# A graph network layer on one core: silu and the exponentials made in another way, one tile in eight groups fetched row by row by SyncE

## The chip, the core and the metric

The kernel runs on one core of a Trainium2 chip, alone. The core has five engines that run side by side, each with its own queue of instructions in a fixed order: TensorE (PE, with PEld for its weight loads), VectorE (DVE), ScalarE (ACT), GpSimd (POOL) and SyncE (SP), which here only starts transfers. Semaphores make one engine wait for another. The metric is the time of one execution on the device in microseconds (us); smaller is better. The kernel before took 3901.85 us, the median of 3 runs (3901.23 to 3902.33).

## What is computed

A graph of 12,500 nodes with 64 features and 412,500 edges with 32 features, the edges sorted by receiver. The reference, cut to what matters:

```python
h = jnp.maximum(_layernorm(x, axis=-1), 0.0)
msg_in = concatenate([h[senders], h[receivers], edge_features], axis=-1)
messages = silu(msg_in @ W1 + b1) @ W2 + b2
att = softmax(silu(msg_in @ Wa1 + ba1) @ Wa2 + ba2, axis=0)     # over all edges
aggregated = segment_sum(messages * att, receivers, num_segments=12500)
return x + silu(concatenate([h, aggregated]) @ Wu1 + bu1) @ Wu2 + bu2
```

All is float32. The softmax runs over all edges at once, so the kernel keeps a running maximum and rescales what it has summed.

## The kernel before

**Nodes first.** The product of `[h[senders], h[receivers], edge] @ [Wa1 | W1]` is split. For each node the senders' part (128 numbers: 64 for attention, 64 for the message) is computed once and written to a table in DRAM, `ts_d`; the receivers' part with the bias goes to `tr_d`. These weights are halved beforehand (L248). The transposed features stay in SBUF as `hT`.

**Edges in groups.** An edge tile is 128 edges, a group is 8 tiles (`K`), and there are 403 groups (`NG`). For each edge, one row of `ts_d` has to be fetched by its sender. The loop over groups (L718 to L784) works on several groups at once; in iteration g:

- `load(g + 2)` (L504) prepares a later group. GpSimd fetches the senders' rows with one indirect transfer for each tile, 128 rows of 512 bytes, into the buffer `gs` (L513; seven such buffers). SyncE fetches every fourth group the edge features `eo` (L524) and receiver numbers `dbs` (L527, two transfers), and for every group a window of `tr_d` around the group's first receiver (`wins`, three buffers, L534, two transfers with an address from a register). VectorE compares the receivers with the rows of the window (L538), and TensorE makes receivers' part and edge part in PSUM, `pe` (L542, three buffers).
- In even groups from 8 to 390 the eighth tile isn't fetched by GpSimd. ScalarE collects it instead: 128 single columns of `hT`, each a copy of 4 bytes in 128 partitions whose address comes from a register (`columns`, L475 to L484), in bursts of 32 after one load of 32 numbers (L479). `burst(g, 0)` and `burst(g, 1)` (L486) give each iteration two bursts, 64 copies. SyncE fetches which half of the column counts (`half`, L472), VectorE masks (L547), and TensorE multiplies with the weights into `pe` (L548).
- `begin(g)` (L550): VectorE adds `pe` to `gs` (L553; in even groups the eighth tile is copied, L555), ScalarE takes the tanh of all 1024 columns (L556), written over `pe`.
- `end(g)` (L558): VectorE makes silu from it, (tanh + 1) times the sum, for the message half into `acts` (L566) and for the attention half (L572), multiplies the latter by `wa2` (L574) and sums to one logit for each edge (L577).
- Four groups make a batch. `top` (L585) finds the batch's maximum with a transpose on TensorE (L596), `weigh` (L599) updates the running maximum `nmax`, and ScalarE makes `scale`, the exponential of the change (L607), and `p`, the exponentials of the batch's logits with their sum (L610). `weigh` of a batch is called in the first iteration of the next one, after `burst(g, 1)` (L748).
- `sum_up` works on a group that lies at least five back: `by_node` (L614) builds for each tile a 128 x 40 matrix with `p` at each edge's receiver (L620, eight instructions) and TensorE sums the messages by receiver (L626); `out_of` (L632), `project` (L637) and `put` (L640 to L659) add the result to the sums of all nodes.

In the groups 16 to 119, beside this, thirteen tiles of nodes are prepared (`tile_bias`, `tile_bias_out`, `tile_rest`, L301 to L358). After the last group the sums become the output (L789 to L871).

**What sets the order.** Most instructions go through `pin`, which keeps an instruction behind the one written before it on the same engine. What isn't pinned (the loads of numbers into registers, most transfers on SyncE and the gathers) a scheduler places when the program is built, as early as it thinks that its inputs are there. What is pinned behind an unpinned load moves with it.

Of the kernel before, what the change touches and what calls it, by code (L numbers as in the profile page):

```python
# [9 lines left out]
I32 = mybir.dt.int32  # L10
# [34 lines left out]
WIDE = 128  # L45
EPS = 1e-5
# [313 lines left out]
def one_pass(tc, n_edges, v):  # L360
# [17 lines left out]
    with ExitStack() as ctx:  # L378
# [43 lines left out]
        with tc.tile_pool(name="work2", bufs=2) as work2, \  # L422
                tc.tile_pool(name="small", bufs=3) as small, \
                tc.tile_pool(name="pre_ps", bufs=AHEAD + 1, space=PSUM) as pre_ps, \
                tc.tile_pool(name="one_ps", bufs=1, space=PSUM) as one_ps:
            pes, gss, lgs, ps_, psums, sps, pps, ees, mts, nums, cols = ({} for _ in range(11))
# [12 lines left out]
            chosen = {g: i for i, g in enumerate(picks)}  # L439
            hT8 = v["hT"].rearrange("d b p -> d (b p)").bitcast(U8)  # L440
            sets = [(i, min(P, len(picks) - i)) for i in range(0, len(picks), P)]
# [3 lines left out]
            def places():  # L445
# [4 lines left out]
                for k, (i, n) in enumerate(sets):  # L450
                    e = (picks[i] * K + K - 1) * EP
                    nc.sync.dma_start(num[:n, k, :], bass.AP(
                        tensor=v["src_row"].tensor, offset=v["src_row"][:, e:].offset,
                        ap=[[EVERY * K * EP, n], [1, EP]]))
# [8 lines left out]
                for k, (i, n) in enumerate(sets):  # L463
                    nc.sync.dma_start(par_d[k * P:k * P + n, :], low[:n, k, :])
# [3 lines left out]
            def numbers(g):  # L468
                if g in chosen:
                    n = nums[g] = small.tile([P, EP], I32, name="half", bufs=3)  # L470
                    row = par_d[chosen[g]:chosen[g] + 1, :]
                    nc.sync.dma_start(n, bass.AP(tensor=row.tensor, offset=row.offset, ap=[[0, P], [1, EP]]))  # L472
                    cols[g] = small.tile([P, EP], F32, name="cols", bufs=3)

            def columns(g, first, n):  # L475
                if g not in chosen:
                    return
                to, i = cols[g].bitcast(U8), chosen[g]
                _, regs = nc.values_load_multi_w_load_instructions(  # L479
                    spots[i % P:i % P + 1, i // P, first:first + n], engines=[ENG.Activation],  # L480
                    min_val=HT_AT, max_val=HT_AT + 2 * NP - 4, skip_runtime_bounds_check_because=WHY)
                for i in range(n):
                    pin(nc.scalar.copy(to[:, 4 * (first + i):4 * (first + i) + 4],  # L483
                                       hT8[:, bass.ds(regs[i] - HT_AT, 4)]))  # L484

            def burst(g, k):  # L486
# [6 lines left out]
            tr_w = bass.AP(tensor=tr_d.tensor, offset=tr_d.offset,  # L493
                           ap=[[C, NP + WR - SHIFT], [SHIFT * C, 2], [1, C]])

            def registers(g, engine, at, base=base_sb, top=NP - 1):
                n = min(NQ, NG + (base is not base_sb) - g)
# [6 lines left out]
            def load(g):  # L504

                t = g * K
                if g % NQ == 0:
                    registers(g, ENG.SP, at_sp)
# [24 lines left out]
                for r in range(2):  # L533
                    nc.sync.dma_start(win[r * R:(r + 1) * R, :, r, :],  # L534
                                      tr_w[bass.ds(at_sp[g], R), :, :])
# [14 lines left out]
            def begin(g):  # L550

                n = K - (g in chosen)
                pin(nc.vector.tensor_tensor(gss[g][:, :n, :], pes[g][:, :n, :], gss[g][:, :n, :], ALU.add))  # L553
                if n < K:
                    pin(nc.vector.tensor_copy(gss[g][:, n, :], pes[g][:, n, :]))  # L555
                pin(nc.scalar.activation(pes[g], gss[g], AF.Tanh))  # L556

            def end(g, then=None):  # L558

                s = batch[g]  # L560
                if g == starts[s]:
                    lgs[s] = small.tile([EP, B * K], F32, name="lg")
                gs, th = gss.pop(g), pes.pop(g)

                def message():
                    pin(nc.vector.scalar_tensor_tensor(acts[g % ACTS][:, :, 0:U], th[:, :, U:C], 1.0,  # L566
                                                       gs[:, :, U:C], op0=ALU.add, op1=ALU.mult))

                if g < NG - 1:
                    message()  # L570
                att = th[:, :, 0:U]
                pin(nc.vector.scalar_tensor_tensor(att, th[:, :, 0:U], 1.0, gs[:, :, 0:U],  # L572
                                                   op0=ALU.add, op1=ALU.mult))
# [3 lines left out]
                pin(nc.vector.tensor_reduce(lgs[s][:, k:k + K], att, AX.X, ALU.add))  # L577
# [4 lines left out]
                if g == NG - 1:  # L582
                    message()

            def top(s):  # L585

                n = size[s] * K
                lg = lgs[s]
# [10 lines left out]
            def weigh(s):  # L599
# [5 lines left out]
                fall = small.tile([P, 1], F32, name="fall")  # L605
                pin(nc.vector.tensor_tensor(fall, nmax[:, s + 1:s + 2], nmax[:, s:s + 1], ALU.subtract))
                pin(nc.scalar.activation(scale[:, s:s + 1], fall, AF.Exp))  # L607
                p = ps_[s] = small.tile([EP, B * K], F32, name="p")
                psum = small.tile([EP, 1], F32, name="psum")
                pin(nc.scalar.activation(p[:, :n], lgs.pop(s)[:, :n], AF.Exp, bias=nmax[:EP, s + 1:s + 2],  # L610
                                         accum_out=psum))
                psums[s] = psum

            def by_node(g):  # L614
# [4 lines left out]
                for j in range(K):  # L619
                    pin(nc.vector.tensor_scalar(wt[:, j, :], iota_w[:EP, j // H, :],  # L620
# [503 lines left out]
```

## Time and profile before

| | |
|---|---|
| median of 3 runs | 3901.85 us |
| the profiled execution | 3904.89 us |
| its span, first to last instruction | 3903.1 us |
| mean granted TensorE clock | 0.642 of full speed |
| GpSimd: 3032 gathers (L513) | 2871.4 us busy |
| ScalarE: 24,576 column copies (L483) | 2415.5 us busy |
| VectorE: all | 3115.4 us busy |
| moved by the transfers | 391.30 MB, 100 GB/s |

Times in the profile are microseconds from the start of the span, or nanoseconds where a mean of one instruction is meant. A row of a group gives line, engine, operation, output and inputs with their shapes, how many; then busy time and mean time of one in ns; then how long the engine stood idle just ahead of them, and what ended that. "issue" means that nothing which the profile shows was waited for. Small instructions overlap, so busy time can be less than count times mean. A row of waits gives who waited for whom: total, times, longest. SPq and ACTq are the queues of SyncE and ScalarE: transfers being started, registers being loaded (TENSOR_LOAD) or computed (MOVE, FUSED_REGOPS).

### The profile page before, as it was taken

How to read it: one execution, taken by the hardware profiler on the slowest of the kernel's cores; microseconds unless marked ns; L12 is line 12 of the kernel's file. 1: busy time of each engine (PE TensorE's matmuls, PEld its weight loads, DVE VectorE, ACT ScalarE, POOL GpSimd, SP SyncE). 2: the span in 40 equal slices, each digit the busy share in tenths (PEclk: the TensorE clock that was granted, in tenths of full speed). 3: DMA queues.
4: the chain of work that ended last, by engine and by line, in shares of the span. 5: the costliest groups of instructions: out<-in, count | busy, mean ns of one | idle time of the engine just before them, and what ended most of it. 6: DMA issues, size and time to landing. Idle time of an engine off the chain costs nothing. (4 is left out here: it accounts for less than half of the span.)

```text
span 3903.1 us, 72226 instructions
## 1 busy us (share of the span) xinstructions
PE 2368.6 (61%) x11368; PEld 1927.2 (49%) x11368; DVE 3115.4 (80%) x8929; ACT 2954.1 (76%) x25797; POOL 2888.6 (74%) x3057
## 2 busy tenths in 40 slices
PE   6566656666666666665665656556565565555655
PEld 5454444454445554554444545445444454444545
DVE  6888787878788888887877877778777777877887
ACT  2887777777778888887877777878877878878712
POOL 3777777777777777777777777777777777777774
PEclk8766566666666657666666666666666666666666
DMA  7433334333433333333333333333333333333343
GB/s 280 114 104 94 102 100 106 94 104 99 107 93 97 97 97 91 94 97 94 87 97 85 97 93 89 97 86 97 93 88 97 86 96 91 90 97 86 95 116 86
DMA packets 228304, 391.30 MB, mean 100 GB/s; under 512 B 72369, under 2 KB 155762, under 8 KB 214770
## 3 DMA queue, kind: packets, MB, share of 16 engines
q0 software_dynamic: 97024, 198.90, 19.5%
q1 hardware_dynamic: 130802, 187.73, 17.9%
q14 instruction: 385, 3.15, 0.3%
q8 instruction: 93, 1.52, 0.2%
HBM read 360.52 MB, written 25.82 MB: 99 GB/s over the span
## 5 line engine op out<-in xcount | busy, mean ns | idle before, releaser
L513 POOL DMA_INDIRECT gs<-ts_d,src_sb x3032 | 2871.4, 947 | 973.1 <-issue 844.2
L483 ACT COPY cols<-hT 128x4 uint8 x24576 | 2415.5, 189 | 595.2 <-issue 594.2
L542 PE MATMUL pe<-wins,eo 128*128 128x256 f32 x3224 | 1470.7, 630 | 846.4 <-DVE eo L538 619.9
L542 PEld LDWEIGHTS pe<-wins,eo 128*128 128x128 f32 x3224 | 964.4, 316 | 1145.4 <-DVE eo L538 708.6
L620 DVE TENSOR_SCALAR wt<-iota_w,dloc,p 128x40 f32<-128x40 f32 x3224 | 726.9, 323 | 1.8
L553 DVE TENSOR_TENSOR gs<-pe,gs 128x1024 f32<-128x1024 f32 (+1 forms) x403 | 467.0, 1159 | 325.7 <-DMA gs<-ts_d,src_sb 303.3
L626 PE MATMUL sp<-wt,acts 128*65 128x40 f32 x6448 | 621.9, 268 | 4.6 <-DVE wt L620 3.5
L626 PEld LDWEIGHTS sp<-wt,acts 128*65 128x65 f32 x6448 | 586.0, 183 | 11.4 <-DVE wt L620 6.2
L556 ACT ACTIVATE pe<-gs 128x1024 f32<-128x1024 f32 x403 | 410.6, 1019 | 215.9 <-DVE gs L553 125.3
L637 PEld LDWEIGHTS mt<-ss,w2u 65*128 65x128 f32 x806 | 201.7, 281 | 330.4 <-issue 291.9
L637 PE MATMUL mt<-ss,w2u 65*128 65x40 f32 x806 | 183.7, 322 | 255.5 <-DVE gm L603 221.4
L566 DVE SCALAR_TENSOR_TENSOR acts<-pe,gs 128x512 f32<-128x512 f32 x403 | 277.6, 689 | 21.6 <-ACT pe L556 12.2
L574 DVE TENSOR_TENSOR pe<-pe,w_all 128x512 f32<-128x512 f32 x403 | 281.8, 699 | 13.5
L572 DVE SCALAR_TENSOR_TENSOR pe<-pe,gs 128x512 f32<-128x512 f32 x403 | 280.3, 696 | 10.5
L596 PE MATMUL mt<-ident,mx 128*128 128x128 f32 x107 | 46.7, 437 | 396.4 <-DVE sums L655 375.9
L577 DVE TENSOR_REDUCE lg<-pe 128x8 f32<-128x512 f32 x403 | 276.7, 687 | 10.5
L538 DVE TENSOR_SCALAR eo<-dbs,bj 64x256 f32<-64x256 int32 x806 | 275.5, 371 | 9.2
L596 PEld LDWEIGHTS mt<-ident,mx 128*128 128x128 f32 x107 | 19.2, 179 | 408.3 <-issue 404.5
L658 DVE COPY stand<-nmax 64x40 f32 x806 | 159.0, 197 | 3.4 <-issue 0.3
L547 DVE SCALAR_TENSOR_TENSOR cols<-half,cols 128x128 f32<-128x128 int32 x192 | 67.1, 349 | 100.6 <-ACT cols L483 98.5
L651 DVE SCALAR_TENSOR_TENSOR sums<-sums,scale,mt 64x40 f32 x214 | 54.4, 254 | 110.9 <-PE mt L637 107.4
L548 PEld LDWEIGHTS pe<-stack,cols 128*128 128x128 f32 x384 | 121.7, 317 | 32.5
(126 smaller groups left out, 957.6 us busy)
## 6 DMA issues: line engine op xcount, KB each, us to landing
eo<-in_edge_dram SPq DMA_DIRECT2D x100, 512.0 KB
dbs<-in_dst_row_dram SPq DMA_DIRECT2D x200, 256.0 KB
gs<-ts_d,src_sb POOLq DMA_INDIRECT x3032
wins<-tr_d SPq DMA_DIRECT2D x806, 32.0 KB
half<-par_d SPq DMA_DIRECT2D x192, 64.0 KB
ts_d<-ts SPq DMA_DIRECT2D x5, 896.0 KB
tr_d<-tr SPq DMA_DIRECT2D x5, 896.0 KB
hT_d<-hT SPq DMA_DIRECT2D x7, 448.0 KB
```

The costliest lines, as they stand in the source:

```text
L483: pin(nc.scalar.copy(to[:, 4 * (first + i):4 * (first + i) + 4], hT8[:, bass.ds(regs[i] - HT_AT, 4)]))
L513: nc.gpsimd.indirect_dma_start(out=full[:rows, j, :], out_offset=None, in_=ts_d[:, :], in_offset=bass.IndirectOffsetOnAxis(ap=src_full[:ro ...
L542: pin(nc.tensor.matmul(pe[:, 2 * q:2 * q + 2, :], eo[:, q * EP:(q + 1) * EP], win[:, q // 2, :, :], start=True, stop=q < H - 1 or g not in ...
L553: pin(nc.vector.tensor_tensor(gss[g][:, :n, :], pes[g][:, :n, :], gss[g][:, :n, :], ALU.add))
L556: pin(nc.scalar.activation(pes[g], gss[g], AF.Tanh))
L566: pin(nc.vector.scalar_tensor_tensor(acts[g % ACTS][:, :, 0:U], th[:, :, U:C], 1.0, gs[:, :, U:C], op0=ALU.add, op1=ALU.mult))
L572: pin(nc.vector.scalar_tensor_tensor(att, th[:, :, 0:U], 1.0, gs[:, :, 0:U], op0=ALU.add, op1=ALU.mult))
L574: pin(nc.vector.tensor_tensor(att, att, wa2[:EP, None, :].to_broadcast([EP, K, U]), ALU.mult))
L577: pin(nc.vector.tensor_reduce(lgs[s][:, k:k + K], att, AX.X, ALU.add))
L620: pin(nc.vector.tensor_scalar(wt[:, j, :], iota_w[:EP, j // H, :], dloc[:, g * K + j:g * K + j + 1], p[:, k + j:k + j + 1], op0=ALU.is_equ ...
L626: pin(nc.tensor.matmul(sp, acts[g % ACTS][:, j, :], wt[:, j, :], start=j == 0, stop=j == K - 1))
L637: pin(nc.tensor.matmul(pp, w2u.rearrange("s h u -> s (h u)"), sps.pop(g), start=True, stop=True))
```

## The change

- `begin` adds the gathered rows into `pe` in PSUM, so that the eighth tile needs no copy, and ScalarE makes silu itself with two instructions of 512 columns: attention into a new tile `att`, message into `acts`. The scale 2.0 undoes the halving. The two multiplications of `end` go.
- `weigh` gets the exponentials from tanh: with t = tanh(x / 32), exp(x / 16) = (1 + t) / (1 - t), and four squarings make exp(x), three on VectorE and the last on ScalarE, which also sums. The change of the maximum is one more column of the same instructions.
- `by_node` builds the matrix of all eight tiles in two instructions (compare, multiply).
- From group 15 on, in every eighth group up to 383 (47 groups, all odd), the last tile isn't gathered by GpSimd. SyncE fetches its 128 rows one by one into a tile `lone`, 16 rows in each iteration from 6 to 381, the last of them two iterations before the group begins. The numbers come into `ids` with a transfer, VectorE multiplies them by 512 (`scaled`), SyncE loads 16 of them into registers at once. All this is pinned. `begin` adds `lone` with an instruction of its own.
- The window's address is a byte offset too: `base_by` holds the first receivers times 512, and a row of the window's source is named by one register.
- A way to let VectorE collect columns as well (`vcolumns`, `spare_columns`, `vpicks`) is written but has nothing to do: `VRES` is empty, so its lists are. It is left out below.

```diff
+ROWS = 16
+ROW0 = 6
...
+            fetched = {}
+            for i in range(NG):
+                g = ROW0 + (EP * (i + 1) - 1) // ROWS + 2
+                if g < NG - 12:
+                    fetched[g] = i
+            order = list(fetched)
+            def ask(i):
+                if i < len(order):
+                    g = order[i]
+                    e = (g * K + K - 1 - (g in chosen)) * EP
+                    ids[i] = small.tile([1, EP], I32, name="ids", bufs=2)
+                    nc.sync.dma_start(ids[i], v["src_row"][:, e:e + EP])
+            def scaled(i):
+                if i < len(order):
+                    pin(nc.vector.tensor_scalar(ids[i], ids[i], 9, None, op0=ALU.logical_shift_left))
+            def fetch(g):
+                at = (g - ROW0) * ROWS
+                end = min(at + ROWS, len(order) * EP)
...
+                while 0 <= at < end:
+                    i, first = at // EP, at % EP
+                    n = min(end - at, EP - first)
+                    if first < ROWS:
+                        ask(i + 1)
+                    if EP // 2 <= first < EP // 2 + ROWS:
+                        scaled(i + 1)
+                    if first == 0:
+                        lone[order[i]] = small.tile([P, C], F32, name="lone", bufs=2)
+                    to = lone[order[i]]
+                    loads, regs = nc.values_load_multi_w_load_instructions(
+                        ids[i][0:1, first:first + n], engines=[ENG.SP], min_val=0, max_val=(NP - 1) * 4 * C,
+                        skip_runtime_bounds_check_because=WHY)
+                    for one in loads:
+                        pin(one)
+                    for k in range(n):
+                        pin(nc.sync.dma_start(to[first + k:first + k + 1, :].bitcast(U8),
+                                          ts8[bass.ds(regs[k], 4 * C)][None, :]))
+                    at += n
...
-                for j in range(K - (g in chosen)):
+                for j in range(K - (g in chosen) - (g in fetched)):
...
-                    nc.sync.dma_start(win[r * R:(r + 1) * R, :, r, :],
-                                      tr_w[bass.ds(at_sp[g], R), :, :])
+                    nc.sync.dma_start(win[r * R:(r + 1) * R, :, r, :].bitcast(U8),
+                                      tr_w[bass.ds(at_sp[g], 1)].rearrange("o r k f -> (o r) k f"))
...
             def begin(g):
-                n = K - (g in chosen)
-                pin(nc.vector.tensor_tensor(gss[g][:, :n, :], pes[g][:, :n, :], gss[g][:, :n, :], ALU.add))
-                if n < K:
-                    pin(nc.vector.tensor_copy(gss[g][:, n, :], pes[g][:, n, :]))
-                pin(nc.scalar.activation(pes[g], gss[g], AF.Tanh))
+                n = K - (g in chosen) - (g in fetched)
+                pe, gs = pes[g], gss.pop(g)
+                pin(nc.vector.tensor_tensor(pe[:, :n, :], pe[:, :n, :], gs[:, :n, :], ALU.add))
+                if g in fetched:
+                    pin(nc.vector.tensor_tensor(pe[:, n, :], pe[:, n, :], lone.pop(g)[:EP], ALU.add))
+                del pes[g]
+                att = atts[g] = silus.tile([P, K, U], F32, name="att")[:EP]
+                pin(nc.scalar.activation(att, pe[:, :, 0:U], AF.Silu, scale=2.0))
+                pin(nc.scalar.activation(acts[g % ACTS][:, :, 0:U], pe[:, :, U:C], AF.Silu, scale=2.0))
...
-                fall = small.tile([P, 1], F32, name="fall")
-                pin(nc.vector.tensor_tensor(fall, nmax[:, s + 1:s + 2], nmax[:, s:s + 1], ALU.subtract))
-                pin(nc.scalar.activation(scale[:, s:s + 1], fall, AF.Exp))
+                lg = lgs.pop(s)
+                pin(nc.vector.tensor_scalar(lg[:, n:n + 1], nmax[:, s:s + 1], -1.0, None, op0=ALU.mult))
+                part = small.tile([P, 1], F32, name="part")
+                pin(nc.vector.tensor_scalar(part, nmax[:, s + 1:s + 2], 1.0 / 32, None, op0=ALU.mult))
+                t, d = (small.tile([P, B * K + 1], F32, name=k)[:, :n + 1] for k in ("t", "d"))
+                pin(nc.scalar.activation(t, lg[:, :n + 1], AF.Tanh, bias=part, scale=1.0 / 32))
+                pin(nc.vector.tensor_scalar(d, t, -1.0, 1.0, op0=ALU.mult, op1=ALU.add))
+                pin(nc.vector.reciprocal(d, d))
+                pin(nc.vector.scalar_tensor_tensor(t, t, 1.0, d, op0=ALU.add, op1=ALU.mult))
+                for _ in range(3):
+                    pin(nc.vector.tensor_tensor(t, t, t, ALU.mult))
                 p = ps_[s] = small.tile([EP, B * K], F32, name="p")
-                pin(nc.scalar.activation(p[:, :n], lgs.pop(s)[:, :n], AF.Exp, bias=nmax[:EP, s + 1:s + 2],
-                                         accum_out=psum))
+                pin(nc.scalar.activation(p[:, :n], t[:EP, :n], AF.Square, accum_out=psum))
+                pin(nc.vector.tensor_tensor(scale[:, s:s + 1], t[:, n:n + 1], t[:, n:n + 1], ALU.mult))
...
-                for j in range(K):
-                    pin(nc.vector.tensor_scalar(wt[:, j, :], iota_w[:EP, j // H, :],
-                                                dloc[:, g * K + j:g * K + j + 1],
-                                                p[:, k + j:k + j + 1],
-                                                op0=ALU.is_equal, op1=ALU.mult))
+                at = dloc[:, g * K:(g + 1) * K].rearrange("p (r h) -> p r h", h=H)
+                pin(nc.vector.tensor_tensor(wt.rearrange("p (r h) w -> p r h w", h=H),
+                                            iota_w[:EP, :, None, :].to_broadcast([EP, 2, H, W]),
+                                            at[:, :, :, None].to_broadcast([EP, 2, H, W]), ALU.is_equal))
+                pin(nc.vector.tensor_tensor(wt, wt, p[:, k:k + K, None].to_broadcast([EP, K, W]), ALU.mult))
...
                 if g + AHEAD < NG:
                     load(g + AHEAD)
+                fetch(g)
                 numbers(g + 6)
```

More of the change, by code (lines that the diff above doesn't have):

```diff
@@ L45 @@
 WIDE = 128
+ROWS = 16
+ROW0 = 6
+VTURN = 4
+VRES = ()
+VSTART = 3
+VLATER = 6
+VBUFS = 2
 EPS = 1e-5
@@ new lines, in one_pass @@
+            order = list(fetched)
+            ids, lone = {}, {}
+            ts8 = ts_d.rearrange("n f -> (n f)").bitcast(U8)
+            def ask(i):
[7 more added lines that the diff above has]
+                    pin(nc.vector.tensor_scalar(ids[i], ids[i], 9, None, op0=ALU.logical_shift_left))
@@ new lines, in one_pass, with registers @@
+            at_sp, at_lo, at_hi, bus, rest = {}, {}, {}, {}, {}
+            row = 4 * C
+            tr8 = tr_d.bitcast(U8)
+            tr_w = bass.AP(tensor=tr8.tensor, offset=tr8.offset,
+                           ap=[[1, (NP - 1) * row + 1], [row, R], [SHIFT * row, 2], [1, row]])
+            base_by = keep.tile([1, NG + 1], I32, name="base_by")
+            nc.vector.tensor_scalar(base_by[:, :NG], base_sb[:, :NG], 9, None, op0=ALU.logical_shift_left)
+            def registers(g, engine, at, base, top):
+                n = min(NQ, NG + (base is not base_by) - g)
@@ L745, in one_pass @@
                     break
+                spare_columns()
+                vcolumns(g, 1)
                 end(g)
```

98 lines of the change are left out of this document (62 added, 36 removed).

## Prediction

> **What bounds the kernel now.** I read the page first, then the waits, then each engine's own rows. The first fence holds the page's span and busy shares, the gather line by itself (minimum, median and longest time, first and last start) and the waits of four engines (total, times, longest).
>
> ```profile
> span 3903.1 us, 72226 instructions
> PE 2368.6 (61%) x11368; PEld 1927.2 (49%) x11368; DVE 3115.4 (80%) x8929; ACT 2954.1 (76%) x25797; POOL 2888.6 (74%) x3057
> ...
> L513 POOL DMA_INDIRECT gs<-ts_d,src_sb x3032: 940/944/1352, 51.7 to 3846.0; - x190
> ...
> POOL gs L513 <- issue: 844.2, 2770, 0.3
> POOL gs L513 <- DMA gs<-ts_d,src_sb: 34.8, 114, 0.3
> ...
> ACT cols L483 <- issue: 594.2, 764, 1.3
> ACT pe L556 <- DVE gs L553: 125.3, 101, 9.6
> ...
> SPq L534 <- PE pe L542: 1251.2, 192, 10.7
> ```
>
> By busy share VectorE leads (80%), but it is GpSimd that never stops: no wait ahead of a gather is longer than 0.3, and "issue" means that nothing else held it. 3032 gathers start between 51.7 and 3846.0, (3846.0 - 51.7) / 3031 = **1.252 us each**. A usual pair of groups needs 15 of them, 9.39 a group. SyncE, in contrast, waits over 1251 for window buffers: it runs far ahead.
>
> The second limit is close. These rows are ScalarE's groups between 1250 and 1500, where it catches up with GpSimd:
>
> ```profile
> L483 ACT COPY cols<-hT 128x4 uint8 x1846 | 181.4, 189 | 35.3 <-issue 35.3
> L556 ACT ACTIVATE pe<-gs 128x1024 f32<-128x1024 f32 x29 | 29.4, 1014 | 0.0
> ```
>
> No wait for another engine is among them, so this is ScalarE at its own pace: 1846 copies are 28.8 groups of 64, and 250 / 28.8 = **8.67 a group**.
>
> **The change part by part.** *Gathers.* One tile leaves GpSimd in each group numbered 15, 23, ... 383, 47 in all. 47 x 1.252 = **58.8 us** less on the engine that sets the pace: 15 gathers a pair become 59 in eight groups, 9.23 a group.
>
> *Single rows.* The 47 x 128 rows go to SyncE, 16 in each of the groups 6 to 381, in its one queue with the windows, halves, edges and numbers. Its rows (minimum, median, longest; then timeline rows with start and time):
>
> ```profile
> L534 SPq FUSED_REGOPS  x806: 37/37/51, 88.1 to 3808.6; - x162
> L534 SPq MOVE wins<-tr_d x806: 29/29/38, 88.1 to 3808.6; - x162
> L534 SPq DMA_DIRECT2D wins<-tr_d x806: 316/317/1870, 88.2 to 3808.7; - x162
> ...
> L472 SPq DMA_DIRECT2D half<-par_d x192: 344/367/551, 94.8 to 3660.9; - x192
> ...
> L524 SPq DMA_DIRECT2D eo<-in_edge_dram x101: 471/481/1662, 79.2 to 3755.2; - x101
> ...
> L527 SPq DMA_DIRECT2D dbs<-in_dst_row_dram x202: 332/416/1281, 79.7 to 3755.8; - x101
> ...
> L498 SPq TENSOR_LOAD <-base_sb x101: 294/301/753, 87.2 to 3774.6; - x101
> ...
> L479 ACTq TENSOR_LOAD <-spots x768: 1942/2008/2800, 98.4 to 3706.6; - x192
> ...
> 7.80 0.31 SPq L148 DMA_DIRECT2D base_sb<-in_first_dram  x1
> ...
> 121.51 0.83 SPq L534 DMA_DIRECT2D wins<-tr_d  x2
> ...
> 3622.38 0.82 SPq L534 DMA_DIRECT2D wins<-tr_d  x2
> ...
> 500.97 1.30 SPq L349 DMA_DIRECT2D xt<-in_x_dram  x2
> ...
> 515.78 1.14 SPq L333 DMA_DIRECT2D bq_d<-bu  x2
> ```
>
> The one-row transfer of base_sb is the nearest to a single row: 0.31. The windows' pair (0.83 for two transfers, one FUSED_REGOPS and one MOVE) leaves about 0.04 between instructions. A single is then 0.31 + a MOVE 0.03 + two gaps: 0.41, as I take it; without the MOVE 0.35, with a FUSED_REGOPS 0.49. The offsets are now bytes, scaled beforehand, so that multiplication has nothing left to do, for the windows either. A group then costs SyncE 16 x 0.41 = 6.56; the load of 16 numbers, between 0.30 for 4 (L498) and 2.01 for 32 (L479), by a straight line 1.03, 1.07 with its gap; windows 0.89; half a half 0.23; a quarter of an edge load, two receiver loads and a number load, 0.49; an eighth of the ids 0.05. Sum **9.30** (8.3 and 10.6 at the two bounds), against 9.23 for GpSimd. SyncE's 1251 us of waiting are used up.
>
> What it is moved past: the windows of group g + 2 stand ahead of group g's rows, so they come late only by what SyncE is late in all. From its group 6 (121.51) to its group 381 (now at 3622.38, three groups ahead of use) it would need 375 x 9.30 = 3488, and some 45 more for the thirteen node tiles' transfers (a pair of xt 1.30, a pair of bq 1.14, one xb, each some 3.2): the windows of 383 go out at 3654, its last rows 9 later, and it can begin at 3665, as now (next fence, first row). GpSimd alone would let it begin at 3607.
>
> *The end.* The last 12 groups take 8 gathers each, 10.0 a group, while the others there are faster. First the tanh of group 383, then all engines from 3720 to 3870 (busy times of PE, PEld, DVE, ACT, POOL; the second last number is the busy share of the DMA queues):
>
> ```profile
> 3665.56 1.03 ACT L556 ACTIVATE pe<-gs 128x1024 f32<-128x1024 f32 x1 [0.37 <-DVE gs L553]
> ...
> 3720.00:3870.00 150.00, 81.06 (x448) 66.43 (x447) 122.15 (x393) 24.78 (x68) 98.60 (x104) 0.63 0.35 101
> ```
>
> VectorE is busy 122.15 for about 14 groups, 8.7 each, and loses some work below; I take 8. GpSimd is ahead by then, so from 383 on there are 7 groups at ScalarE's 8.8, 12 at 8 and 52 of ending (57 now from the last gather's start to the end, less 5 for its landing and addition), 210 instead of today's 238: 3665 + 210 = 3875.
>
> *Arithmetic.* The rows (times in ns of one, the second number behind the bar) that price the rest:
>
> ```profile
> L574 DVE TENSOR_TENSOR pe<-pe,w_all 128x512 f32<-128x512 f32 x403 | 281.8, 699 | 13.5
> L572 DVE SCALAR_TENSOR_TENSOR pe<-pe,gs 128x512 f32<-128x512 f32 x403 | 280.3, 696 | 10.5
> L566 DVE SCALAR_TENSOR_TENSOR acts<-pe,gs 128x512 f32<-128x512 f32 x403 | 277.6, 689 | 21.6 <-ACT pe L556 12.2
> L620 DVE TENSOR_SCALAR wt<-iota_w,dloc,p 128x40 f32<-128x40 f32 x3224 | 726.9, 323 | 1.8
> L555 DVE COPY gs<-pe 128x128 f32<-128x128 f32 x192 | 53.9, 281 | 0.0
> L831 ACT ACTIVATE mt<-hT 128x512 f32<-128x512 f32 x4 | 2.4, 597 | 1.8 <-POOL hT L826 1.6
> L556 ACT ACT_TABLE_LOAD x1 | 1.3, 1283 | 49.5 <-DVE gs L553 49.5
> L610 ACT ACTIVATE p<-lg,nmax 128x32 f32<-128x32 f32 x98 | 30.0, 306 | 0.0
> L607 ACT ACTIVATE scale<-fall 128x1 f32<-128x1 f32 x107 | 21.3, 199 | 33.7 <-DVE fall L606 33.7
> L589 DVE TENSOR_TENSOR lg<-lg,w_all 128x32 f32<-128x32 f32 x98 | 18.9, 193 | 3.3
> L208 DVE RECIPROCAL rstd<-rstd 128x14 f32<-128x14 f32 x5 | 1.2, 239 | 2.0 <-ACT rstd L203 1.9
> L208 DVE RECIPROCAL rstd<-rstd 128x8 f32<-128x8 f32 x2 | 0.4, 196 | 1.3 <-ACT rstd L203 1.3
> L691 DVE SCALAR_TENSOR_TENSOR total<-total,scale,psum 128x1 f32<-128x1 f32 x107 | 23.1, 216 | 15.4 <-ACT p L610 13.5
> ```
>
> VectorE loses the two multiplications of silu (0.69 + 0.70), half a copy (0.14) and eight small weights (726.9 / 403 = 1.80); it gains two of 320 elements (by L574's rate about 0.50 each), the lone tile and the scaling (0.28 each, an eighth). That is 2.3 less a group, before the weighing adds 0.4, and nothing on the path. ScalarE makes two silus of 512 (0.60 each, overlapping by 0.1) for one tanh of 1024 (1.01): 0.08 more a group, 8.75.
>
> *The weighing*, once in four groups, is where cover can go. Now two exponentials stand in a row on ScalarE and VectorE goes on. Afterwards tanh (behind a burst of 32 copies) is followed by seven VectorE operations and the Square waits for them: 0.19 + reciprocal of 33 (196 and 239 for 8 and 14 give 0.38) + 0.22 + 3 x 0.19, with 0.03 between, 1.55 us. Queued behind the waiting VectorE instruction is the next group's addition (1.2), for which the next silu waits: another 1.1 of ScalarE. Uncovered, 2.7 in four groups with the longer first activation, 0.7 a group: 8.75 + 0.7 = 9.45, over GpSimd's 9.23. What may cover it is the next burst of copies, which doesn't depend on any of this and isn't pinned behind it (each burst begins with a number load that is unpinned). That bursts do move ahead shows at the start:
>
> ```profile
> 98.98 1.03 ACT L556 ACTIVATE pe<-gs 128x1024 f32<-128x1024 f32 x1
> ...
> 102.78 3.13 ACT L483 COPY cols<-hT 128x4 uint8 x32
> ```
>
> That is a burst right behind the tanh of group 0, though the first that the program writes with anything to do belongs to group 4. I count the weighing at nothing, with 0.7 a group as its upper bound.
>
> *A rule weighed.* The row says 0.31 on SyncE for any transfer. The Trainium skill, "DMA: Bandwidth & Descriptors", section "Anatomy of one DMA", gives about 50 ns to a sequencer's dispatch (for GpSimd's path); by it, as an estimate, SyncE would need some 5 a group and the answer would be GpSimd's alone. No transfer of this trace was issued in that time, so I keep the row.
>
> **Forecast.** GpSimd alone ends at 3903.1 - 58.8 = 3844; SyncE's sum gives 3875. The profiled execution took 3904.89, 1.8 over its span and 3.0 over the median of 3901.85, so on the median these are 3843 and 3874. I forecast **3866**: faster by 0.9%, SyncE nearly the limit. Each 0.1 in SyncE's 9.30 is 37 us once it decides. Below 3843 only a quicker gather would help, for which nothing is changed; 944 ns is the median, 940 the least.
>
> **Rivals.**
> 1. *SyncE becomes the bound* and the kernel is slower. The price is its time per group, the place its queue, the point 9.38 a group, where 3875 becomes 3903. At 9.5, if it also waits 0.2 a group for its own earlier transfers (edge and receiver loads), 3949; with 0.49 a single 4350. For it: a sum with a margin of minus 0.07. Against: the unused 1251 us, and that it begins three groups ahead.
> 2. *ScalarE becomes the bound* through the uncovered weighing: 9.45 a group, 0.06 over today's 9.39, for 383 groups 23; 25 node tile steps, in which VectorE now has no lead left, about 1.5 each, 37; less 25 at the end: 3902 + 35 = 3937. It binds from 1.9 us of stall per weighing on, (9.23 - 8.75) x 4. A second form of it: if silu and tanh are not served by one table, two loads of 1283 (L556) per weighing, 2.6 more, give about 4000. The Trainium skill, "ScalarE: Activation LUTs", section "Table sets", lists tanh beside exp and sigmoid and says nothing of silu; this trace can't show it.
> 3. *The gain is lost in the queues*: the freed gathers come, but the others slow, since 6016 small rows share their 16 DMA queues. 2% on 1.252 is 75 us: 3918. Little speaks for it: queues 35% busy (the row from 3720), and 128 rows in eight groups replace as many.
>
> **How the numbers follow.** Forecast 0.48 (its own range 3840 to 3897), SyncE 0.26, ScalarE 0.17, lost gain 0.09. About 0.2%, 8 us, is what a measurement of this kernel can tell from no change. Of the forecast 0.44 is faster and 0.04 the same; of the rest 0.03 faster, 0.06 the same, 0.43 slower. So 0.47 faster, 0.10 same, 0.43 slower. The range reaches from 3838 to 3990, over the ScalarE case and SyncE up to 9.6; it leaves out SyncE well beyond, the table loads, and what is quicker than GpSimd.
>
> **What would show it.** 2985 gathers at 1.25, from about 52 to 3790; single rows at 0.41 and number loads near 1.0 on SyncE; ScalarE's copies between tanh and Square; VectorE near 2400 busy. I am wrong if GpSimd shows waits for buffers in the middle of the span, if the matrix products wait for windows, or if ScalarE stands idle ahead of each Square.

## The result, and the profile after

The changed kernel takes **4008.19 us** (median of 4 runs, 4006.39 to 4009.79), the kernel before 3902.09 beside it: a ratio of **1.027, 95% interval 1.026 to 1.028**. It is slower by 106 us; 3866 was forecast, in a range that ended at 3990. Two limits turned out to stand one behind the other: each weighing stops ScalarE, which sets the pace, and VectorE's new instructions hold up the gathers, which takes the gain away behind it. In some later sessions the kernel before itself took 5870 to 6020 us, and times measured there are not compared with the others.

First the page of the changed kernel, then from two more views its gather line (minimum, median and longest time, first and last start) and the waits of four engines (total, times, longest):

```profile
span 4004.7 us, 80328 instructions
...
PE 2294.9 (57%) x11368; PEld 1816.2 (45%) x11368; DVE 2368.1 (59%) x6464; ACT 2970.9 (74%) x26201; POOL 2914.7 (73%) x3010
```

```profile
L602 POOL DMA_INDIRECT gs<-ts_d,src_sb x2985: 938/944/1464, 52.0 to 3929.0; - x199
```

```profile
POOL gs L602 <- issue: 838.3, 2587, 49.6
POOL gs L602 <- DVE pe L643: 94.2, 83, 2.5
```

```profile
ACT cols L498 <- issue: 544.5, 763, 2.0
ACT att L648 <- DVE pe L643: 185.8, 125, 6.1
ACT p L705 <- DVE t L702: 175.6, 106, 3.2
```

```profile
DVE d L695 <- ACT t L693: 520.4, 104, 5.7
```

```profile
SPq L623 <- PE mt L733: 219.0, 89, 7.8
SPq L616 <- DVE eo L627: 197.0, 79, 13.0
```

VectorE lost a quarter of its work, and 47 gathers are gone, yet the last one starts 83 us later than before. GpSimd now waits 83 times for VectorE's addition, since that frees its buffers; before, once the gathers ran, no wait of it was longer than 0.3. Counted in the two traces at 2500, the gathers are six groups ahead of the additions now, with seven buffers, and were one group ahead before: GpSimd has stopped being the limit. New in ScalarE's list are 106 waits of the Square for the last squaring, 1.66 each, and 186 us ahead of the silu where 125 stood ahead of the tanh. SyncE still waits for others: it is not the limit.

One weighing, in the order of ScalarE's rows (start, time, what; idle time ahead and what ended it):

```profile
2411.56 0.59 ACT L648 ACTIVATE att<-pe 128x512 f32<-128x512 f32 x1
...
2420.09 0.59 ACT L648 ACTIVATE att<-pe 128x512 f32<-128x512 f32 x1
2420.58 0.58 ACT L649 ACTIVATE acts<-pe 128x512 f32<-128x512 f32 x1
2421.06 0.18 ACT L728 COPY ss<-sp 65x40 f32<-65x40 f32 x1
2421.45 3.14 ACT L498 COPY cols<-hT 128x4 uint8 x32 [0.21 <-issue]
2425.57 3.14 ACT L498 COPY cols<-hT 128x4 uint8 x32 [0.98 <-issue]
2428.62 0.32 ACT L693 ACTIVATE t<-lg,part 128x33 f32<-128x33 f32 x1
2430.64 0.23 ACT L705 ACTIVATE p<-t 128x32 f32<-128x32 f32 x1 [1.70 <-DVE t L702]
2430.78 0.19 ACT L705 ACTIVATION_READ_ACCUMULATOR p<-t 128x1 f32 x1
2432.28 0.60 ACT L648 ACTIVATE att<-pe 128x512 f32<-128x512 f32 x1 [1.32 <-DVE pe L643]
```

From silu to silu an ordinary group takes 8.5, this one 12.2. No copies stand between tanh and Square: both bursts are already through. VectorE's and GpSimd's rows of the same moment:

```profile
2428.97 0.32 DVE L695 TENSOR_SCALAR d<-t 128x33 f32<-128x33 f32 x1 [5.45 <-ACT t L693]
...
2431.02 1.23 DVE L643 TENSOR_TENSOR pe<-pe,gs 128x1024 f32<-128x1024 f32 x1 [0.21 <-DMA gs<-ts_d,src_sb]
```

```profile
2433.00 1.20 POOL L602 DMA_INDIRECT gs<-ts_d,src_sb  x1 [2.47 <-DVE pe L643]
```

VectorE stands idle for 5.45, because its first instruction of the second half waits for the tanh, which stands behind 32 copies; so the addition comes late, and GpSimd stands idle for 2.47 until it has its buffer. (The transfer named beside the addition can't be what it waited for: the gathers were six groups ahead.) Over the stretch from 1300 to 3500, behind the node tiles (means worked out from ScalarE's rows), ordinary groups take 8.49, groups with a weighing 12.12, and the one behind it 9.32, as its number load comes late: (2 x 8.49 + 12.12 + 9.32) / 4 = **9.60 a group**, for GpSimd's 9.39 before.

The second thing is in the gathers. By shape, with the mean time in ns behind the bar's comma, before and after:

```profile
L513 POOL DMA_INDIRECT gs<-ts_d,src_sb x3032 | 2871.4, 947 | 973.1 <-issue 844.2 <-DMA ts_d<-ts 49.3 <-DMA gs<-ts_d,src_sb 34.8
```

```profile
L602 POOL DMA_INDIRECT gs<-ts_d,src_sb x2985 | 2897.5, 971 | 1030.1 <-issue 838.3 <-DVE pe L643 94.2 <-DMA gs<-ts_d,src_sb 57.6
```

The median is 944 in both, but fewer gathers take more time in all. One of the long ones, and what VectorE does when it starts:

```profile
2613.76 0.94 POOL L602 DMA_INDIRECT gs<-ts_d,src_sb  x1 [0.30 <-issue]
2615.01 1.42 POOL L602 DMA_INDIRECT gs<-ts_d,src_sb  x1 [0.30 <-DVE wt L719]
2616.73 0.94 POOL L602 DMA_INDIRECT gs<-ts_d,src_sb  x1 [0.30 <-issue]
```

```profile
2614.52 0.49 DVE L719 TENSOR_TENSOR wt<-wt,p 128x320 f32<-128x320 f32 x1
2614.93 0.69 DVE L659 TENSOR_TENSOR att<-att,w_all 128x512 f32<-128x512 f32 x1
2615.65 0.69 DVE L662 TENSOR_REDUCE lg<-att 128x8 f32<-128x512 f32 x1
```

The multiplication of L659 still has 0.61 to run when the gather starts, and the gather takes 0.48 longer. The 390 gathers that start 0.05 or more after L659, L716 or L719 has begun, while it runs, follow one line: 0.944 plus what the instruction has left, less 0.1 (left 0.30 to 0.35: mean 1.147; 0.60 to 0.65: 1.430; less than 0.1: 0.944). They carry 53 of the 80 us that all gathers take over 0.944 each. Of the rest, 10 lie on 76 gathers that start within the first 0.05, of which most take their usual time, and 16 on the others, mostly those that start up to 0.5 ahead of L716. All three instructions read two operands from SBUF; before, the multiplication read silu from PSUM and each weight took one SBUF tensor and two scalars.

Which of the two sets the pace can be worked out: gathers of 0.971 with 0.305 between them need 7.375 x 1.276 = 9.41 a group, under ScalarE's 9.60. So the weighing is the limit here, and the slower gathers would be the next one.

### The profile page after: what moved, and what is told of

It reads as the page before. It is cut to its first block, busy times and chain, and to the rows that moved or that the text cites. A ratio compares the mean times of both kernels' runs of the same rounds, so it can differ in the third digit from the quotient of the medians.

```text
span 4004.7 us, 80328 instructions
## 1 busy us (share of the span) xinstructions
PE 2294.9 (57%) x11368; PEld 1816.2 (45%) x11368; DVE 2368.1 (59%) x6464; ACT 2970.9 (74%) x26201; POOL 2914.7 (73%) x3010
## 5 line engine op out<-in xcount | busy, mean ns | idle before, releaser
L631 PE MATMUL pe<-wins,eo 128*128 128x256 f32 x3224 | 1345.3, 590 | 1048.4 <-DVE eo L627 1010.4
L631 PEld LDWEIGHTS pe<-wins,eo 128*128 128x128 f32 x3224 | 917.2, 298 | 1291.7 <-DVE eo L627 1069.1
L643 DVE TENSOR_TENSOR pe<-pe,gs 128x896 f32<-128x896 f32 (+1 forms) x403 | 463.2, 1149 | 60.0 <-DMA gs<-ts_d,src_sb 39.6
L659 DVE TENSOR_TENSOR att<-att,w_all 128x512 f32<-128x512 f32 x403 | 277.5, 689 | 198.3 <-ACT att L648 197.9
L648 ACT ACTIVATE att<-pe 128x512 f32<-128x512 f32 x403 | 237.8, 590 | 192.7 <-DVE pe L643 185.8
L695 DVE TENSOR_SCALAR d<-t 128x33 f32<-128x33 f32 (+2 forms) x107 | 27.3, 255 | 520.4 <-ACT t L693 520.4
L662 DVE TENSOR_REDUCE lg<-att 128x8 f32<-128x512 f32 x403 | 275.0, 682 | 10.6
L649 ACT ACTIVATE acts<-pe 128x512 f32<-128x512 f32 x403 | 234.8, 583 | 0.0
L637 PE MATMUL pe<-stack,cols 128*128 128x128 f32 x384 | 106.0, 364 | 178.1 <-DVE cols L636 177.9
L719 DVE TENSOR_TENSOR wt<-wt,p 128x320 f32<-128x320 f32 x403 | 199.4, 495 | 13.9
L716 DVE TENSOR_TENSOR wt<-iota_w,dloc 128x320 f32<-128x320 f32 x403 | 195.1, 484 | 1.6
L705 ACT ACTIVATE p<-t 128x32 f32<-128x32 f32 (+2 forms) x107 | 24.3, 227 | 175.6 <-DVE t L702 175.6
```

Source lines behind the costliest of these rows:

```text
L631: pin(nc.tensor.matmul(pe[:, 2 * q:2 * q + 2, :], eo[:, q * EP:(q + 1) * EP], win[:, q // 2, :, :], start=True, stop=q < H - 1 or g not in ...
L643: pin(nc.vector.tensor_tensor(pe[:, :n, :], pe[:, :n, :], gs[:, :n, :], ALU.add))
L648: pin(nc.scalar.activation(att, pe[:, :, 0:U], AF.Silu, scale=2.0))
L649: pin(nc.scalar.activation(acts[g % ACTS][:, :, 0:U], pe[:, :, U:C], AF.Silu, scale=2.0))
L659: pin(nc.vector.tensor_tensor(att, att, wa2[:EP, None, :].to_broadcast([EP, K, U]), ALU.mult))
L662: pin(nc.vector.tensor_reduce(lgs[s][:EP, k:k + K], att, AX.X, ALU.add))
```

## The experiments

Theory **W**: ScalarE's stop at each weighing sets the pace. Theory **G**: the instructions with two SBUF operands slow the gathers. Rival **S**: the single rows, in SyncE's queue or beside the gathers, are the cause. Ratios are to the kernel before on the same chip, with 95% intervals.

**1. Tanh ahead of the second burst (early_tanh).**

```diff
                 end(g)
+                if batch[g] and g == starts[batch[g]] and weighed[0] <= batch[g] - 1:
+                    weigh_first(batch[g] - 1)
                 burst(g, 1)
                 if batch[g] and g == starts[batch[g]]:
                     weigh_upto(batch[g] - 1)
```

weigh_first holds the weighing up to the tanh, weigh_upto now the rest of it.

> The changed kernel with one thing moved: the tanh of a weighing goes out ahead of the second burst of copies, its Square stays behind it, so that VectorE's seven instructions between the two run beside 32 copies. Theory W (ScalarE waits at each weighing, 12.13 us for that group instead of 8.49, and the next number load comes late, 9.33): ScalarE falls to some 8.75 a group, and the time falls. How far tells W from W+G. Theory G (gathers of the changed kernel are slower, 971 ns in the mean for 947, because VectorE's new instructions with two SBUF inputs hold them up): GpSimd then needs 7.375 x 1.276 = 9.41 a group, as before, and the time is about 3910. W alone (gathers back at 1.252): 3845. Theory S (the single rows in SyncE's queue set the pace): unchanged, 4000 or more.

Measured: 3929.59, ratio 1.006 (1.005 to 1.008). ScalarE's waits ahead of the Square and VectorE's ahead of its first instruction fall from 175.6 and 520.4 to:

```profile
ACT p L715 <- DVE t L712: 18.9, 11, 3.0
```

```profile
DVE d L705 <- ACT t L695: 117.2, 98, 2.5
```

GpSimd hardly waits for buffers any more and sets the pace again, but its gathers still take 971 each:

```profile
L602 POOL DMA_INDIRECT gs<-ts_d,src_sb x2985 | 2899.5, 971 | 959.2 <-issue 899.1 <-DMA gs<-ts_d,src_sb 20.1 <-DVE mx L677 5.5
```

So W is worth 79 us here, and what is left, 3930 instead of 3845, is for G to explain. The groups now take 9.42 (1300 to 3500), as 7.375 gathers of 1.276 do.

**2. No large instruction with two SBUF operands (one_sbuf).**

```diff
-                att = atts[g] = silus.tile([P, K, U], F32, name="att")[:EP]
+                att = atts[g] = pe[:, :, 0:U]
...
-                pin(nc.vector.tensor_tensor(wt..., ALU.is_equal))
-                pin(nc.vector.tensor_tensor(wt, wt, p..., ALU.mult))
+                for j in range(K):
+                    pin(nc.vector.tensor_scalar(wt[:, j, :], iota_w..., dloc..., p...,
+                                                op0=ALU.is_equal, op1=ALU.mult))
```

> The changed kernel without large VectorE instructions that read two SBUF operands: the attention half of silu stays in PSUM, where it is multiplied, and the weights are made by eight instructions of one SBUF tensor and two scalars each, as before the change. The weighing stays as it is. Theory G: the gathers go back to 947 ns in the mean, and nearly none is over 1.05 us. The time: W says ScalarE still sets 9.6 a group, so 3990 to 4020 in spite of quick gathers. If G were the cause by itself, 3845 to 3870. Theory S: gathers stay slow, 4000.

Measured: 4433.59, 1.135 (1.133 to 1.137). The gathers are as G says, the time is a miss:

```profile
L602 POOL DMA_INDIRECT gs<-ts_d,src_sb x2985 | 2824.3, 946 | 1511.9 <-issue 905.1 <-DVE pe L643 532.5 <-DVE sums L751 49.7
```

```profile
2405.29 0.57 ACT L648 ACTIVATE pe<-pe 128x512 f32<-128x512 f32 x1
2405.90 0.60 ACT L649 ACTIVATE acts<-pe 128x512 f32<-128x512 f32 x1
2406.39 0.18 ACT L728 COPY ss<-sp 65x40 f32<-65x40 f32 x1
2407.95 3.14 ACT L498 COPY cols<-hT 128x4 uint8 x32 [1.38 <-issue]
2412.01 3.14 ACT L498 COPY cols<-hT 128x4 uint8 x32 [0.92 <-issue]
2415.06 0.57 ACT L648 ACTIVATE pe<-pe 128x512 f32<-128x512 f32 x1
```

The edit had a side effect. As both silus now work in one PSUM tile, the second waits for the first; the number load behind it starts only with the second silu (at 2405.91 in the trace) and, hidden but for 0.21 in the changed kernel, costs 1.38: an ordinary group is 9.8 instead of 8.5, before any weighing.

**3. Both edits (early_one_sbuf), and then the number loads pinned 20 copies early (best_p20).**

```diff
-                _, regs = spots_of(g, first, n, ENG.Activation)
+                regs = ahead.pop((g, first), None) or numbered(g, first, n)
+                at = calls.index((g, first, n))
                 for i in range(n):
+                    if i == n - 20 and at + 1 < len(calls):
+                        ahead[calls[at + 1][:2]] = numbered(*calls[at + 1])
```

numbered is the load with its instructions kept in program order, calls the list of bursts.

> Both edits together. W+G: GpSimd is the limit again with 7.375 gathers of 1.252, 9.23 a group: 3840 to 3860, faster than both kernels. If SyncE is the limit at the 9.3 of the prediction, 3875 or more. Theory S: 4000.

> The changed kernel with the early tanh and without the large instructions of two SBUF operands, and with ScalarE's number loads pinned 20 copies ahead of the burst that uses them. In the run with the first two edits alone the number loads had moved, so that ScalarE stood 1.38 and 0.92 us before the bursts of each group (9.87 a group for 8.5). If that is the only reason it was slow: ScalarE falls below 8.5 a group, GpSimd is the limit with 7.375 x 1.252 = 9.23, and the time is 3840 to 3860. If VectorE's longer chain (eight weights again, 2.6 us for 1.0) is the reason: 4000 or more.

Measured: 4114.88, 1.053 (1.051 to 1.055), and 3966.93, 1.015 (1.013 to 1.017). Both miss. The gathers take 945 and 946, but ScalarE sets the pace: the median group takes 9.87 and 9.43 (1300 to 3500). In best_p20 each of the two loads of a group costs 1.0, since only copies of 0.1 stand ahead of it:

```profile
2411.76 1.24 ACT L511 COPY cols<-hT 128x4 uint8 x12
2413.99 3.14 ACT L511 COPY cols<-hT 128x4 uint8 x32 [1.00 <-issue]
2418.11 2.00 ACT L511 COPY cols<-hT 128x4 uint8 x20 [0.98 <-issue]
```

These runs show G in the gathers, not yet in the time.

**4. The rows by themselves: the changed kernel without them (no_rows), the kernel before with nothing but them (rows_only).**

```diff
-                if g < NG - 12:
+                if g < 0:
                     fetched[g] = i
```

is no_rows; rows_only is the kernel before with the change's fetch(g), its byte addresses of the windows, and in begin(g)

```diff
+                if g in fetched:
+                    pin(nc.vector.tensor_tensor(gss[g][:, n, :], pes[g][:, n, :], lone.pop(g)[:EP], ALU.add))
+                    n += 1
```

> The changed kernel without the single rows: all 3032 gathers on GpSimd again, everything else as changed. W: ScalarE's 9.61 is above GpSimd's 7.5 x 1.276 = 9.57, so about the same, 4000 to 4015. Theory S: the rows were the cause, and without them the time falls to about 3910.

> The kernel before with one part of the change: the single rows on SyncE (47 tiles leave GpSimd) with the windows' addresses in bytes; tanh, exponentials, weights and their operands stay as before. Theory G+W: the gain of the rows is real, and what lost it came from the other parts. Gathers stay at 947 ns in the mean, 1.252 apart; GpSimd needs 9.23 a group, and the time is 3845 to 3875. If the rows themselves slow the gathers or SyncE is the limit: 3900 or more.

Measured: no_rows 4011.26, 1.027 (1.025 to 1.028), as the changed kernel; **rows_only 3859.81, 0.988 (0.986 to 0.990)**, faster than both kernels. S falls. (In no_rows GpSimd needs 7.5 x 1.280 = 9.60 a group, no more than ScalarE, so the 47 gathers that it has again don't show in the time.) The gathers of rows_only, by shape and between 2500 and 3000 (busy time and count):

```profile
L566 POOL DMA_INDIRECT gs<-ts_d,src_sb x2985 | 2824.2, 946 | 973.1 <-issue 896.5 <-DMA gs<-ts_d,src_sb 17.4 <-DVE wt L676 12.5
```

```profile
2500.00:3000.00 500.00, 377.99 (x401) 0.62 0.40 95
```

401 in 500 us, 1.25 each: in this stretch the rows beside them slow nothing.

**5. One instruction more with two SBUF operands (extra_two), and one with a single one (extra_one).** In the kernel with the early tanh, in a tile `idle` whose result nobody reads:

```diff
                 end(g)
+                pin(nc.vector.tensor_tensor(idle, dloc[:, :K * C], dloc[:, K * C:2 * K * C], ALU.add))
```

for extra_two, and for extra_one

```diff
+                pin(nc.vector.tensor_reduce(idle[:, :K], dloc[:, :K * C].rearrange("p (k c) -> p k c", k=K), AX.X, ALU.add))
```

> The kernel with the early tanh, and one more VectorE instruction a group whose result nobody reads: an addition of two parts of an SBUF tile, 128 x 1024, some 1.2 us. VectorE has 40% to spare. Theory G (a gather that is to start while such an instruction runs waits for its end, less 0.1): some 0.5 us a group more on GpSimd, gathers of 1.04 us in the mean, time some 4120. Without G: as the next kernel, 3920 to 3950.

> The control to the kernel with an additional addition: in the same place a sum over 128 x 1024 elements, with a single SBUF operand and about the same 1.2 us. Theory G: gathers as without it, 971 ns in the mean, and the time 3920 to 3950. If any longer VectorE work slows the gathers: as the addition, some 4120.

Measured: 4182.05, 1.071 (1.069 to 1.073), and 3924.83, 1.004 (1.003 to 1.006). VectorE's additional instruction and the gathers, of the first and then of the second:

```profile
L858 DVE TENSOR_TENSOR idle<-dloc 128x1024 f32<-128x1024 f32 x402 | 487.8, 1214 | 0.0
```

```profile
L603 POOL DMA_INDIRECT gs<-ts_d,src_sb x2985 | 3159.6, 1058 | 958.9 <-issue 916.4 <-DMA gs<-ts_d,src_sb 20.4 <-DVE t L713 14.0
```

```profile
L858 DVE TENSOR_REDUCE idle<-dloc 128x8 f32<-128x1024 f32 x402 | 485.1, 1207 | 0.0
```

```profile
L603 POOL DMA_INDIRECT gs<-ts_d,src_sb x2985 | 2908.9, 975 | 958.7 <-issue 890.4 <-DMA gs<-ts_d,src_sb 23.5 <-DVE att L660 8.0
```

The same 1.21 us on an engine with 40% to spare: 257 us dearer with two SBUF operands, and GpSimd's busy time shows 3159.6 - 2908.9 = 251 of them. It is also dearer than the 4120 expected. The two differ in one more thing: the addition writes 1024 numbers in each partition to SBUF, the sum 8. That the writing isn't the cause can be seen in rows_only, whose addition reads one operand from SBUF and one from PSUM, writes as much to SBUF and takes as long:

```profile
L606 DVE TENSOR_TENSOR gs<-pe,gs 128x1024 f32<-128x1024 f32 x164 | 200.8, 1224 | 80.1 <-DMA gs<-ts_d,src_sb 54.3 <-issue 21.1 <-PE pe L595 3.9
```

The 354 gathers that start while L606 runs, in either of its two sizes, take 0.944 in the mean, 0.961 at most. So extra_two and extra_one show G by itself, in the time.

**6. The weights in two steps by themselves (rows_wt2_c): rows_only, with the two tensor_tensor of the change for wt.**

> The kernel before with the single rows and the weights in two steps, once more, since in both runs so far the kernel before took some 6000 us. Theory G: gathers near 957 ns instead of 946, 0.08 to 0.12 a group, so 3890 to 3910 instead of the 3860 without the two steps, in spite of less work on VectorE; without G 3860 or less.

Measured: 3880.41, 0.995 (0.993 to 0.996): 21 us slower than rows_only, 27 by the two ratios, and less than the 30 to 50 that were expected. VectorE has 0.8 a group less to do (busy rows of 1.80 and 0.98). The gathers are as expected:

```profile
L566 POOL DMA_INDIRECT gs<-ts_d,src_sb x2985 | 2859.8, 958 | 960.3 <-issue 899.8 <-DMA gs<-ts_d,src_sb 20.8 <-DVE gs L611 8.6
```

**7. What stays open.** Three more edits were made: the early tanh with eight weights (early_wt8), and rows_only with 18 or 20 rows a group.

> The kernel with the early tanh, and the weights again in eight instructions with one SBUF tensor each; the attention half of silu stays in SBUF, where it is multiplied with two SBUF operands (0.69 us). Theory G: by the rule that a gather waits for the rest of the instruction, less 0.1, the two steps of the weights cost 2 x 0.39 x 0.39 / 2.5 = 0.12 of the 0.26 a group that the three cost together; so gathers near 957 ns in the mean instead of 971, GpSimd about 9.32 a group, and the time 3885 to 3900 instead of 3930. If the weights had no part in it: 3930 or more, since VectorE's chain is 1.6 us longer.

> The kernel before with 20 single rows a group instead of 16: 59 tiles leave GpSimd, 12 more. If SyncE still had room, 12 x 1.25 = 15 us are gained, 3845. By the rows of the run with 16, SyncE needs 8.35 a group (a single takes 0.32 with its MOVE, 16 numbers 1.15), and four more make 9.64, over GpSimd's 9.2: then SyncE is the limit and the time is 3950 to 4020, with matrix products that wait for windows.

> The kernel before with 18 single rows a group: 53 tiles leave GpSimd, 6 more than with 16. SyncE at 8.35 + 2 x 0.32 = 9.0 a group stays under GpSimd's 9.21: 6 x 1.25 = 7.5 us less than with 16 rows, about 3852. If SyncE needs 0.2 a group more than its own rows say, it is the limit by now: 3860 to 3900.

All their runs (three of early_wt8, three with 20 rows, one with 18), and two more of rows_wt2, fell into the sessions named with the result, so their times (6033 to 6051; 6519 to 6632; 6711; 5858 and 5869) say nothing of the usual kernel. What can be read there is the gather: 955 to 957 ns in three runs of early_wt8, as G expected, 949 and 951 in rows_wt2, less than the 957 expected, and 945 to 948 with 18 and 20 rows. With 20 rows the matrix products waited for windows there,

```profile
PE pe L595 <- DMA wins<-tr_d: 2633.5, 250, 18.6
```

so SyncE's transfers came late there. From how many rows on SyncE sets the pace in usual times isn't settled. How much of G belongs to the attention product and how much to the weights is shown in the time for the weights alone, by experiment 6. And no run shows in the time what the changed kernel would gain from quick gathers alone, since one_sbuf slowed ScalarE as well.

## Why the prediction was wrong

*What bounds the kernel, and the gathers.* Right. With the rows alone the kernel takes 3860. That this is 6 under the forecast of 3866 is in part luck: 3866 was taken between 3843 (GpSimd alone) and 3874, and the second came from a sum for SyncE that was too large. Of the 58.8 us, 48 arrive in the span (3903.1 to 3855.2). The rest goes at 13 gathers between 947 and 1180, while node tiles are prepared; GpSimd stands idle up to 3.0 ahead of them, 12.6 us in all beyond the usual 0.3. One of them in rows_only:

```profile
1102.36 0.94 POOL L566 DMA_INDIRECT gs<-ts_d,src_sb  x1 [3.00 <-ACT cols L485]
```

No such wait stands in the trace of the kernel before. What makes them late isn't shown.

*SyncE's sum.* The size was off: 9.30 a group was forecast, the rows add up to some 8.3 with the gaps between them (1300 to 3500).

```profile
L571 SPq MOVE lone<-ts_d x6016: 29/29/38, 117.0 to 3758.6; - x195
L571 SPq DMA_DIRECT2D lone<-ts_d x6016: 224/228/335, 117.0 to 3758.6; - x195
```

```profile
L565 SPq TENSOR_LOAD <-ids x376: 972/1168/1239, 115.9 to 3752.4; - x188
```

A single is 0.228 + 0.029 + two gaps, 0.32, not 0.41; the one-row load of base_sb was a poor model. The load of 16 numbers, 1.17 for 1.03, was near. Rival 1 didn't come about: some 8.3 stays under GpSimd's 9.23.

*The weighing.* **The step that failed first: "I count the weighing at nothing, with 0.7 a group as its upper bound."** The cover didn't exist: the one burst seen behind the tanh of group 0 was taken as the scheduler's habit, and 93 of the 98 long weighings stand behind both bursts, with no copy between them and the next silu. The trace before could have told: 95 of its long weighings stand in the same place, behind 64 copies and right ahead of the next tanh. The working of the upper bound was sound for the two waits (1.55 and 1.1 forecast, 1.70 and 1.32 in the weighing shown), but it wasn't a bound: a weighing costs (12.12 - 8.49) + (9.32 - 8.49) = 4.46, 1.1 a group. Of that some 3.0 are the two waits, 0.65 the tanh and the Square, and 0.83 the number load that comes late afterwards, for which the prediction had no term. Against it, ScalarE is otherwise quicker than the 8.75 that the prediction set: 8.49 in an ordinary group, 8.65 with tanh and Square spread over four. Rival 2 named place and mechanism; its 3937 came from 9.45 a group, where 9.60 was measured. Experiment 1 shows the cause: moving one instruction on ScalarE takes 79 us off the median. The second form of this rival, table loads, didn't come about: three stand in the whole trace of the changed kernel, whose loop alternates silu and tanh 98 times, so the two share a table here. The Trainium skill, "ScalarE: Activation LUTs", section "Table sets", lists tanh beside exp and sigmoid and doesn't name silu. Two of the signs that the prediction gave for being wrong came: GpSimd waits for buffers in the middle of the span, and ScalarE stands idle ahead of each Square.

*Arithmetic on VectorE.* **The second step that failed: "That is 2.3 less a group ... and nothing on the path"**, and with it the 1.252 for each gather in the sum, left as it was. Duration was counted, operands weren't. Silu's attention half moved from PSUM to SBUF and the weights became a comparison and a product of SBUF tensors, and GpSimd paid: 75 us between the gathers of rows_only and those of early_tanh (2824.2 and 2899.5), 14 of them in waits that were there anyway (973.1 and 959.2). That is more than the 48 that the rows bring. Rival 3 had such a loss (2% on each gather, 75 us) but blamed the DMA queues; rows_only shows that they do nothing. The Trainium skill, "SBUF — State Buffer", section "Who interferes with whom", states that a VectorE instruction with two SBUF inputs contends with a GpSimd instruction that reads SBUF. The traces agree: gathers, whose numbers lie in SBUF (`src_sb`), take 971 ns for 946, and 1058 with one more such instruction. It is the rule that speaks against this change, and the prediction didn't weigh it.

*The sum, in spans of the profiled executions:* 3903.1, less 47.9 for the rows (3855.2, rows_only), plus 63.5 for the rest of the change with the weighing covered (3918.7, early_tanh), plus 86.0 for the weighing as written (4004.7). The last 86 are 69 up to the last gather's start (3860.2 to 3929.0) and 17 behind it; by the medians they are 79, since the profiled execution of early_tanh was the quickest of its four. The terms hold in this order alone: while the weighing sets the pace at 9.60 a group, quicker gathers (9.23 for 9.41) find no time to save.

## What to carry to other kernels

Before an instruction is moved on an engine that "has time to spare", look at where its operands lie and who else needs that memory: here an instruction with two SBUF operands on VectorE made GpSimd's gathers wait for most of what it had left to run. An exchange across two engines, there and back within one small step, needs work placed between its halves by hand; cover that the scheduler gave once, at the start, isn't cover. When two limits lie close together, mending the first shows only what the second allows. And an undone edit may move other things: the attempts to mend the kernel by its operands were lost to number loads that were hidden no longer.

## What was not expected of the hardware

A gather that starts during a VectorE instruction with two SBUF operands, 0.05 or more after its begin, takes 0.944 plus the rest of that instruction less 0.1; during a sum over one SBUF operand it takes its usual time (394 gathers of extra_one: 0.945 in the mean). A number load of ScalarE (2.0 us) is hidden all but 0.21 behind two silus, unless a wait holds it back (1.02 behind a weighing, 1.38 in one_sbuf), and leaves 0.9 to 1.0 behind copies of 0.1 each, with 12 or with 32 of them behind the silus; so moving it ahead within a run of copies doesn't hide it. SyncE issues a one-row transfer every 0.32.
